# A two-layer recurrent model on one core: the gathers and joins of the second experts' rows move to later steps of the second attention

## Chip, core and metric

The kernel runs on one core of a Trainium2 chip. The metric is the device time of one execution in microseconds (us). The kernel before took 707.73 us, the median of three runs (707.6 to 710.62).

## What is computed

Two layers, one after the other, on x of shape (4, 512, 128), all in float32. Each layer normalises x, computes an attention s and a mixture of experts, turns the latter into a gate g, and adds s * g to x. The change lies in the second layer, where the experts' gate is brought together while the attention runs:

```
xn = layernorm(x)
s = L1_attn(xn, ...)            # 16 heads of 8, 16 channels of softmax attention, keys 512
g = silu(L1_ffn(xn, ...))       # each token: the two experts of largest probability out of 8
x = x + s * g

# L1_ffn, per token n:
probs = softmax(gelu(xt @ wg1 + bg1) @ wg2)
top_vals, top_idx = top_k(probs, 2)
h = gelu(einsum('nd,edh->enh', xt, w_in));  o = einsum('enh,ehd->end', h, w_out)
y[n] = sum over the token's two experts e of gate[n, e] * o[e, n]
```

## The kernel before

The tokens are four batches (b = 0 to 3) of 512, each held as a tile of 128 partitions by four groups of 128 columns (k = 0 to 3). Batch 0 runs through all eight experts densely. For batches 1 to 3 the kernel sorts tokens into rooms, one per expert, computes only the chosen experts, and writes the results as rows to a scratch table in DRAM (`rows[b]`). What comes back to each token are two rows: that of its first expert and that of its second.

`fetch(b, at)` (L1114 to L1127) brings them back. For each b there are eight gathers, at = 0 to 7, each an indirect DMA issued by GpSimd (POOL) of 128 rows of 512 bytes, one row per partition. The first four fill `g` (the first expert's rows), the last four a second tile (`first` for batch 1, `xnT` for batches 2 and 3). `joined(b, part)` (L1129 to L1135) combines them on VectorE (DVE): part 0 multiplies the first tile by its gates, part 1 the second tile by its gates, part 2 adds the two. The sum is what `gate1` (L1164) later turns into silu, and that is multiplied onto the attention's output of the same batch in `output1` (for batch 3 in `end1`).

The second attention, `attn1` (L1962), is a loop of 64 steps, i = 16 * b + t. Step i does the matmuls over one block of 128 keys of one group of four heads (`over_keys`, tile acc), evaluates the exponential and its square for step i + 1 on ScalarE (ACT) with some squares moved to DVE, and issues the scores of step i + 2 (tile s). Into the gaps it places the preparation of the following batches (projections, tiles pl, pf, feat, lin) and the mixing of finished groups (`bank1`, `sums1`, `quotients1`, `output1`, tiles b, den, mix, po). In this loop nearly everything is put on its engine in the order in which the program calls it: `mm1`, `act1`, `vec1`, `pool1` and `dma1` all pin the instruction. So an instruction that waits holds up all behind it on the same engine.

The steps that matter here:

- Whatever is in the dictionary `rest` for step i is called first in step i. It holds nothing but `fetch` and `joined`.
- What a chunk has left for DVE after its matmuls (its "rest") is called one step after the chunk's matmuls were issued. `quotients1(b - 1, 1, 0)` has its matmuls in step t = 5 and its two DVE products (L1722, tile pr) in step t = 6; `quotients1(b - 1, 1, 1)` has them in t = 6 and t = 7. Both pairs of matmuls write the tile mix, of which there are two buffers, so the second pair waits until the first pair's products have been read out by DVE.
- In step t = 4 of batch 2 (i = 36) the third part of `prepare1(3)`'s cubes and its forms (tile pl) are issued; the cubes' six DVE instructions (L1496 to L1508, tile feat) run in step 37.
- In step t = 3 the query projection of the next batch is split into three bf16 parts on POOL (L1463, L1465, tiles partq and leftq).

Before the change, batch 2's gathers stand in steps 20 to 27 and its join in steps 33 to 35; batch 3's gathers stand in steps 28 to 35 and its join in steps 50 to 52. Batch 1's are issued and joined before the loop.

Of the kernel before, what the change touches and what calls it, by code (L numbers as in the profile page):

```python
# [108 lines left out]
class Kernel:  # L109
# [2271 lines left out]
    def run(self):  # L2381
# [96 lines left out]
                self.ffn1(first, between, True)  # L2478
                third.close()
        rest = {}  # L2480
        for b, at, then in ((2, 20, 33), (3, 28, 50)):
            for k in range(8):
                rest.setdefault(at + k, []).append((first.fetch, b, k))
            for k in range(3):
                rest.setdefault(then + k, []).append((first.joined, b, k))
# [67 lines left out]
```

## Time and profile before

The profiled execution took 707.65 us, of which 705.7 us lie between its first and last instruction. The TensorE clock granted was 0.991 on the mean, and 1.00 in every stretch of ten microseconds from 420 to 700 us.

| Engine | busy, us | share of span | instructions |
|---|---|---|---|
| PE (matmul) | 662.5 | 94% | 10120 |
| DVE | 498.5 | 71% | 1072 |
| ACT | 488.9 | 69% | 809 |
| POOL | 344.7 | 49% | 383 |

| Stretch of the second attention, us | PE | DVE | ACT | POOL | DMA share |
|---|---|---|---|---|---|
| 510 to 520 | 9.98 | 8.90 | 10.00 | 8.87 | 0.49 |
| 520 to 530 | 9.48 | 9.86 | 7.85 | 8.81 | 0.47 |
| 560 to 570 | 10.00 | 10.00 | 9.03 | 6.80 | 0.72 |
| 580 to 590 | 9.60 | 9.34 | 10.00 | 7.57 | 0.68 |
| 620 to 630 | 9.90 | 7.99 | 9.03 | 3.51 | 0.27 |
| 640 to 650 | 9.07 | 8.66 | 8.90 | 1.60 | 0.87 |

How to read it: PE is a record of matmul instructions whose ends are modelled, DVE, ACT and POOL are busy times of those engines, each in us out of ten. "DMA share" is the mean busy share of the core's 16 DMA engines. An "issue" in the lists below is time in which an engine waited for nothing that the profile shows. POOL's issues of the gathers appear as DMA_INDIRECT of line L1124: their duration is the time POOL spends on the issue, not the time until the rows have arrived.

The loop's first step begins near 424 us and the last ends near 690 us, so a step takes some 4.2 us.

### The profile page before, as it was taken

Reading aid. Unit: us, or ns where it says so; the run is one execution under the profiler, and the core shown is the slowest. Engines: PE = TensorE matmul, PEld = TensorE weight load, DVE = VectorE, ACT = ScalarE, POOL = GpSimd, SP = SyncE. Lnnn points to the kernel's source line nnn. Section 1 sums busy time; section 2 is a strip of 40 time slices with the busy share of each in tenths; the row PEclk is TensorE's granted clock in tenths of the full one; section 3 lists DMA queues with packets and bytes.
Section 4 is the critical chain, followed back from the end, with each engine's and each line's share of the span. In section 5 each row is a group of like instructions: output and inputs, shape, how many; then the busy total and the mean of one; then the engine's idle time right before and its main releaser. Section 6 shows DMA issues by size and latency. Waiting matters only on the chain.

```text
span 705.7 us, 23780 instructions
## 1 busy us (share of the span) xinstructions
PE 662.5 (94%) x10120; PEld 412.4 (58%) x10123; DVE 498.5 (71%) x1072; ACT 488.9 (69%) x809; POOL 344.7 (49%) x383
## 2 busy tenths in 40 slices
PE   7999899999999799789999999999999999999995
PEld 3666667977977768767787783332335243422324
DVE  6866375676677567874459223989897999678884
ACT  4533477786876877742553468989997899899850
POOL 7670046667677384783753333411383835230170
PEclk9999999999999998999999999999999999999999
DMA  7740252232232222100034249967949494947300
GB/s 166 161 136 0 69 144 86 55 108 78 63 95 75 63 61 64 33 3 1 1 109 147 75 150 218 260 167 171 242 153 210 115 249 143 217 136 179 76 17 20
DMA packets 85489, 79.72 MB, mean 113 GB/s; under 512 B 42640, under 2 KB 74160, under 8 KB 82304
## 3 DMA queue, kind: packets, MB, share of 16 engines
q1 hardware_dynamic: 82544, 75.39, 40.4%
q0 software_dynamic: 2256, 2.47, 1.8%
q8 instruction: 82, 1.34, 0.8%
q10 hardware_dynamic: 576, 0.26, 0.1%
q14 instruction: 31, 0.25, 0.1%
HBM read 51.62 MB, written 26.21 MB: 110 GB/s over the span
## 4 chain that ended last, share of the span: by engine, by line
PE 65%; ACT 14%; DVE 12%; DMA 3%; issue 2%; SPq 1%; POOL 0%; DVEq 0%; ACTq 0%; POOLq 0%
PE acc L336 10%; ACT e L339 8%; PE eo L336 7%; PE pp L336 7%; PE po L336 5%; PE ph L336 4%; PE b L336 3%; PE s L336 3%; PE pl L336 3%; DMA vd<-vt 2%; PE pg L336 2%; PE pu L336 2%; PE den L336 2%; PE sc L336 1%; DVE elu L689 1%
## 5 line engine op out<-in xcount | busy, mean ns | idle before, releaser
L339 ACT ACTIVATE e<-s 128x1024 f32<-128x1024 f32 x124 | 121.9, 1055 | 14.0 <-PE s L336 12.9
L336 PE MATMUL acc<-e,strip 128*32 128x512 f32 x1000 | 124.5, 598 | 0.9 <-DVE e L1946 0.9
L339 ACT ACTIVATE e<-e 128x1024 f32<-128x1024 f32 x104 | 107.3, 1094 | 0.0
L743 POOL TENSOR_TENSOR t<-t,gate 128x512 f32<-128x512 f32 x32 | 50.2, 1567 | 54.9 <-DVE t L724 54.9
L336 PEld LDWEIGHTS acc<-e,strip 128*32 128x32 f32 x1000 | 28.4, 109 | 70.0 <-issue 58.3
L781 POOL TENSOR_TENSOR t<-t,gate 128x512 f32<-128x512 f32 x32 | 49.6, 1551 | 34.2 <-DVE sums L780 27.7
L689 DVE SCALAR_TENSOR_TENSOR elu<-elu,up 128x512 f32<-128x512 f32 x60 | 46.3, 771 | 11.6 <-ACT up L339 11.4
L339 ACT ACTIVATE pj<-pp 128x512 f32<-128x512 f32 x64 | 38.0, 608 | 15.4 <-PE pp L336 14.1
L339 ACT ACTIVATE h<-ph 128x1024 f32<-128x1024 f32 x20 | 20.5, 1024 | 39.0 <-PE ph L336 32.3
L336 PE MATMUL s<-q,k 64*128 64x512 bf16 x256 | 40.9, 382 | 3.6 <-ACT e L339 3.3
L782 POOL TENSOR_TENSOR t<-t,t 128x512 f32<-128x512 f32 x32 | 42.7, 1333 | 2.5
L336 PEld LDWEIGHTS <-k 64*128 64x128 bf16 x256 | 8.7, 94 | 59.7 <-issue 58.6
L666 DVE TENSOR_TENSOR E<-sc,cap 128x512 f32<-128x512 f32 x32 | 22.0, 688 | 29.5 <-PE sc L336 29.5
L336 PE MATMUL eo<-w_out,h 128*128 128x128 f32 x320 | 39.7, 278 | 0.0
L336 PEld LDWEIGHTS eo<-w_out,h 128*128 128x128 f32 x320 | 37.6, 192 | 3.4 <-issue 2.2
L339 ACT ACTIVATE elu<-pj 128x512 f32<-128x512 f32 x60 | 38.6, 643 | 0.1
L339 ACT ACTIVATE up<-pj 128x512 f32<-128x512 f32 x60 | 38.4, 640 | 0.0
L1727 POOL TENSOR_TENSOR pr<-pr,pr 128x512 f32<-128x512 f32 x14 | 22.6, 1633 | 29.7 <-DVE pr L1722 29.6
L336 PE MATMUL pp<-xnT,l0Wk 128*64 128x128 f32 x512 | 33.4, 289 | 2.4 <-ACT sk L339 1.6
L339 ACT ACTIVATE attT<-tn 128x128 f32<-128x128 f32 x100 | 19.5, 282 | 21.4 <-PE tn L702 20.5
L1634 DVE TENSOR_TENSOR second<-second,first 128x1024 f32<-128x1024 f32 x16 | 27.0, 1693 | 8.7 <-DMA second<-qf 7.3
L336 PEld LDWEIGHTS pp<-xnT,l0Wk 128*64 128x64 f32 x512 | 30.5, 146 | 4.2 <-ACT sk L339 2.6
(346 smaller groups left out, 1590.3 us busy)
## 6 DMA issues: line engine op xcount, KB each, us to landing
vd<-vt SPq DMA_DIRECT2D x32, 256.0 KB
vone<-vd SPq DMA_DIRECT2D x64, 128.0 KB
first<-qe SPq DMA_DIRECT2D x8, 1024.0 KB
second<-qf SPq DMA_DIRECT2D x16, 512.0 KB
third<-qf SPq DMA_DIRECT2D x32, 256.0 KB
qf<-qT SPq DMA_DIRECT2D x64, 64.0 KB
k<-kd SPq DMA_DIRECT2D x16, 256.0 KB
q<-qd SPq DMA_DIRECT2D x16, 256.0 KB
```

The source lines that it names most:

```text
L336: return self.pin(self.nc.tensor.matmul(*args, **kw))
L339: return self.pin(self.nc.scalar.activation(*args, **kw))
L666: self.vec1(nc.vector.tensor_tensor(e, ps[:, :, 0:256].rearrange("p x (hp c) -> p x hp c", hp=4), bc(bc(self.cap, 1, 4), 1, 2), ALU.min,))
L689: self.vec1(nc.vector.scalar_tensor_tensor(t, t, 1.0, up, ALU.min, ALU.add))
L743: nc.gpsimd.tensor_mul(t, t, self.gate)
L781: nc.gpsimd.tensor_mul(t, t, gate2)
L782: nc.gpsimd.tensor_add(t, t, seg[n]["t1"])
L1634: self.vec1(self.nc.vector.tensor_mul(t, t, self.first1[mm][:, two]))
L1727: self.nc.gpsimd.tensor_add(self.prod1[b, m], self.prod1[b, m], t)
```

## The change

One line of `run` changes: the tuples (batch, first step of its gathers, first step of its join).

```diff
         rest = {}
-        for b, at, then in ((2, 20, 33), (3, 28, 50)):
+        for b, at, then in ((2, 28, 37), (3, 44, 53)):
             for k in range(8):
                 rest.setdefault(at + k, []).append((first.fetch, b, k))
             for k in range(3):
                 rest.setdefault(then + k, []).append((first.joined, b, k))
```

Batch 2's gathers move from steps 20 to 27 to steps 28 to 35, its join from 33 to 35 to 37 to 39. Batch 3's gathers move from 28 to 35 to 44 to 51, its join from 50 to 52 to 53 to 55. No instruction is added or removed, and no tile changes its size.

In the built program POOL's order changes so: steps 20 to 27 hold no gather; in steps 28 to 35 batch 2's eight stand in exactly the places where batch 3's stood, the last one behind the five instructions that split batch 3's query projection (L1463, L1465); batch 3's first gather stands ahead of `gate1` of batch 2 (L1168), the next three behind `output1` of batch 1 (L1748), the last four behind the pair of sums L1727 that follows. On DVE, batch 2's part 0 stands between the product on tile third (L1645) and the six cubes instructions of step 37, part 1 between these and the first products pr (L1722) of step 38, part 2 between the next L1645 and the second products pr of step 39. Batch 3's parts 0 and 1 stand next to each other ahead of the products pr of step 54, part 2 ahead of those of step 55. PE, ACT and the order of SP's DMAs are as before.

## The prediction

> **What bounds the kernel now.** First the page's chain that ended last, by engine:
>
> ```profile
> PE 65%; ACT 14%; DVE 12%; DMA 3%; issue 2%; SPq 1%; POOL 0%; DVEq 0%; ACTq 0%; POOLq 0%
> ```
>
> POOL, which issues the gathers, is not on it. TensorE is, and DVE in places, so I ask where DVE decides, and whether the moved joins land there. The same chain in order of time for 580 to 592 us (start, us, what), and DVE's timeline there (start, us, engine, line, operation; in brackets idle time before and its releaser):
>
> ```profile
> 580.92 1.51 PE pl L336 x64
> 582.43 0.02 issue
> 582.45 2.16 DVE feat L1496
> ...
> 585.37 2.40 DVE feat L1508 x3
> 587.76 0.60 DVE pr L1722
> ...
> 588.41 1.72 PE mix L336 x4
> ```
>
> ```profile
> 580.55 1.27 DVE L1645 SCALAR_TENSOR_TENSOR third<-second,count,third 128x1024 f32<-128x1024 f32 x1
> 582.45 2.16 DVE L1496 TENSOR_TENSOR feat<-tokk,feat 128x1024 f32<-128x1024 f32 x1 [0.63 <-PE pl L336]
> ```
>
> This is steps 37 and 38. Six cubes instructions and a product pr run back to back on DVE, and PE's second mix stands behind that pr. After it PE goes without a gap to 617 us. So whatever DVE does between 582.45 and 587.76 moves the end. Exactly there the change puts batch 2's parts 0 and 1.
>
> Third, when part 1's rows arrive. Their last gather takes the place of batch 3's last one; POOL's timeline:
>
> ```profile
> 586.46 0.69 POOL L1463 CAST partq<-leftq 128x512 bf16<-128x512 f32 x1
> 587.30 0.98 POOL L1124 DMA_INDIRECT xnT<-rows,ids  x1 [0.15 <-issue]
> ```
>
> Its rows' packets show in stretches of a quarter of a microsecond (busy PE, PEld, DVE, ACT, POOL, clock, DMA share, GB/s). The clearest case is the last gather before the loop, issued at 395.88 us with little traffic around; the second pair belongs to the gather at 587.30:
>
> ```profile
> 397.25:397.50 0.25, 0.07 (x2) 0.00 (x0) 0.00 (x0) 0.25 (x2) 0.00 (x0) 1.00 0.00 0
> 397.50:397.75 0.25, 0.01 (x1) 0.00 (x0) 0.00 (x0) 0.25 (x1) 0.00 (x0) 1.00 0.81 246
> ```
> ```profile
> 588.75:589.00 0.25, 0.25 (x2) 0.00 (x0) 0.25 (x2) 0.25 (x1) 0.25 (x1) 1.00 0.32 74
> 589.00:589.25 0.25, 0.25 (x3) 0.24 (x2) 0.25 (x1) 0.25 (x1) 0.25 (x1) 1.00 1.97 184
> ```
>
> 246 GB/s for 0.25 us is 61 KB, the 64 KB of one gather: packets run 1.62 to 1.9 us after the issue starts, near 589.25 for the other. DVE reaches the spot at 587.76. **The rows come too late for it.**
>
> **The change, part by part.**
>
> *Part 1 of batch 2 waits (step 38).* The packets' end is not yet the semaphore. At the kernel's start two loads of 64 KB end near 2.9 us, and the first DVE instruction that waits for one starts at 3.34, so I add 0.5 (between 0.4 and 0.8): a gather can be used 1.95 + 0.5 = 2.45 us after its issue starts. The Trainium skill, "DMA: Bandwidth & Descriptors", section on the anatomy of a SWDGE DMA, gives 2.0 us fixed plus bytes over 436 GB/s, which for 64 KB would be an estimated 2.15 us; by it the wait is 0.3 shorter. I take the row.
>
> *Part 0 (step 37).* Each join is one product of 0.68 us (rows L1131: 0.68, 0.68, 0.69 when undisturbed). It stands behind the L1645 that ends at 581.82, in the 0.63 us for which DVE waits for pl: by that, 0.05 lost. But POOL splits the query then, and "SBUF — State Buffer", section "Who interferes with whom", says that a DVE instruction with two SBUF inputs and a POOL instruction reading SBUF exclude each other. The trace has it: L1131 took 1.64 us at 570.31 beside POOL's leftk, and L1496 2.16 at 582.45 against 1.21 at 566.04. If part 0 is served between the first cast and the first subtraction, both queues behind it shift by about 0.65. I take 0.65, with 0 and 1.0 as ends.
>
> *Sum at step 38.* Gather issue 587.30 + 0.65 = 587.95; usable at 587.95 + 2.45 = 590.40; part 1 itself 0.60 from start to start, so pr starts at 591.0 in place of 587.69: **+3.3 us**. Without part 0's shift and with the skill's figure it is 587.30 + 2.15 + 0.60 - 587.69 = +2.4; with part 0 at 1.0, and the issue held up by DVE as at 530.87 us (1.97 in place of 0.98), +4.6. Had the rows been there, part 1 would cost 0.6 alone. Behind the waiting instruction stand both pr pairs, sizes and all of DVE; PE's mix waits for the first pr, and acc, the scores and ACT's next exponentials wait behind mix. ACT can run on for some 4 us (it holds one step of scores) and then waits too. PE and then ACT (617 to 623) are the chain behind it, so nothing absorbs the loss.
>
> *Part 2 (step 39)* adds 0.6 between L1645 (589.72) and pr (590.91). The pr behind it frees mix for pf, 4.8 us after the first pr; with 0.6 more it is done after some 4.5. Cost 0, but only 0.3 us of cover.
>
> *What leaves steps 33 to 35.* Three joins (564.84, 570.31, 574.62), while PE runs without a gap and is the chain: 0.
>
> *What leaves steps 50 to 52.* Here DVE is the chain:
>
> ```profile
> 638.97 1.13 DVE first L1643
> 640.10 0.60 DVE xnT L1131
> 640.70 1.67 DVE inv L1695
> ...
> 642.45 1.15 DVE e L1946
> 643.59 0.04 issue
> 643.64 1.05 PE acc L336 x4
> ```
>
> Batch 3's part 1 leaves it: -0.6. Part 0 (633.74) stood before 1.71 us of waiting for den: 0. Part 2 (643.49) stood where ACT takes over: 0. ACT's gap there is 1.10 us, so the gain ends at 1.1; beyond it ACT is late next. **-0.6.**
>
> *What enters steps 53 to 55.* Parts 0 and 1 follow the L1645 that ends at 647.40; DVE then waits 1.34 us for mix (to 648.73). 2 x 0.68 = 1.36 fits: 0. Part 2 stands before the pr of 653.08; ACT is the chain from 645.97 to 657.25 and DVE waits 0.35 at 657.23 and 1.55 at 660.00: 0, or 0.3 at most. Its rows, last issued by about 634 us, have 13 us.
>
> *POOL and DMA.* Eight gathers leave 515 to 530 us, eight enter between 610 and 634. Alone one takes 0.95, with 0.30 between (386.90 to 396.8): 8 x 1.25 = 10 us. The SBUF page of the skill, section "SBUF: two separate sides", speaks against them: the descriptors of such a DMA can't be written while DVE holds the shared port, and this stretch of DVE is 80% busy; the worst here is 1.97, so 18 us. POOL was idle 16.57, 2.61, 5.65 and 13.92 us before its instructions from 610.76 to 642.59; th and L1764 have that cover, so 0 by either. If a gather did delay th, y would follow, but its output is only stored. The half megabyte goes where the DMA share was 0.27 (620 to 630 us); the tables loaded from 629.5 on are first used at 646.12 (third). SP's order is unchanged. In steps 28 to 35 one batch replaces the other, gather for gather.
>
> **Sum:** 3.3 - 0.6 = +2.7, on 707.65 us (the execution profiled, 0.08 under the median of 707.73): 710.35. I forecast **710.3**, own range 709.3 to 712.0.
>
> **Rivals.**
>
> *Not slower: the gathers slowed PE.* PE loses 0.52 us at 521.92, then 1.66 in b and 0.55 in acc (527.79 to 532.9): 2.7 us that no releaser explains.
>
> ```profile
> 527.79 2.72 PE L336 MATMUL b<-third,lin 64*32 64x512 f32 x16
> 530.45 2.47 PE L336 MATMUL acc<-e,strip 128*32 128x512 f32 x16
> ```
>
> Elsewhere these take 1.06 and 1.92. Nine gathers are issued from 515.27 to 532.84, and PE's gaps at 397.31 and 397.96 follow the last of batch 1's. Against it: the gathers from 552.96 to 564.6 have no such mark, and a gap of 0.67 at 85.97 has no gather near. If the gathers are the cause, 2.7 comes back: 707.65 + 2.7 - 2.7 = 707.7. It decides as soon as it returns more than 2.7; with the rows early as well (cost 0.6 + 0.05, not 3.3) 705.0. Chance 0.19.
>
> *Clearly slower: the gather meets a full DMA.* kd's parts, issued until 572.91, let POOL go on only at 581.32, under a DMA share of 1.0: 8.4 us instead of 2.45, so +6 more, 716. The share at 588 to 590 is 0.72, and 0.26 afterwards, which speaks against it. It decides from 1 us of extra landing time (711.3). Chance 0.25, mostly for 1 to 3 us.
>
> *The wait is hidden:* DVE reaches part 1 later or the rows come sooner; then only 0.65 + 0.6 - 0.6 remain: 708.3. Chance 0.11.
>
> The forecast keeps 0.45. What a measurement here can tell from no change is about 0.5%, or 3.5 us: 704.2 to 711.3. Forecast, hidden wait and most of PE's recovery fall within it; slower are the full-DMA case and the forecast's upper end (0.03). Faster is PE's recovery with early rows (0.05), so same is 0.67, slower 0.28. The range for 8 in 10: 707.0 to 713.5.
>
> **What will show it.** Right: DVE idle about 2 us before xnT L1131 near 588.4, released by a DMA; PE's mix about 3.3 later than 588.41, everything to 636 shifted equally, 0.6 won back at acc near 643.64. Wrong: xnT L1131 without idle time before it, or PE's b near 527 at 1.06 per tile.

## The result, and the profile after

The changed kernel took 711.52 us in the median of 19 runs (709.86 to 714.23); the kernel before, measured beside it, took 707.56 us (19 runs, 704.96 to 710.62). The ratio is 1.0062, with a 95% interval from 1.005 to 1.0074: about 4 us slower. The profiled execution of the changed kernel took 711.52 us, 709.5 of them span, against 707.65 and 705.7 before.

The page's chain that ended last, by engine, after the change. DMA stood at 3% before:

```profile
PE 61%; ACT 15%; DVE 13%; DMA 5%; issue 3%; POOL 1%; SPq 1%; DVEq 0%; ACTq 0%; POOLq 0%
```

Where the new share lies is seen in the same chain in order of time, of the changed kernel (start, us, what), up to the matmuls of step 38:

```profile
568.51 11.37 DMA kd<-partk
...
584.35 0.69 POOL partq L1463
585.04 0.15 issue
585.20 3.51 DMA xnT<-rows,ids
...
588.82 0.69 DVE xnT L1131
589.52 0.61 DVE pr L1722
...
590.17 2.67 PE mix L336 x4
592.84 3.15 PE acc L336 x16
```

Before, this stretch was DVE work without a gap. Now it runs through a transfer that POOL's split of the query waits for (kd, 11.37 us, the larger part of the new DMA share), the split, the last gather (3.51 us) and part 1 of the join. DVE's timeline of the changed kernel shows the wait itself (in brackets the idle time before and who ended it):

```profile
579.31 1.10 DVE L1131 TENSOR_TENSOR g<-g,gates 128x512 f32<-128x512 f32 x1
580.67 1.84 DVE L1496 TENSOR_TENSOR feat<-tokk,feat 128x1024 f32<-128x1024 f32 x1 [0.27 <-PE pl L336]
...
583.19 2.47 DVE L1508 TENSOR_TENSOR feat<-tokk,feat 128x256 f32<-128x256 f32 x3
588.82 0.69 DVE L1131 TENSOR_TENSOR xnT<-xnT,gates 128x512 f32<-128x512 f32 x1 [3.17 <-DMA xnT<-rows,ids]
589.43 1.28 DVE L1722 TENSOR_TENSOR pr<-bank,mix 128x512 f32<-128x512 f32 x2
```

Two rows of PE's timeline hold what nothing in the prediction answers to. First the two rows before the change, then those of the changed kernel:

```profile
588.41 1.72 PE L336 MATMUL mix<-inv,to_mix 64*128 64x512 f32 x4 [0.40 <-DVE pr L1722]
590.06 1.92 PE L336 MATMUL acc<-e,strip 128*32 128x512 f32 x16
```
```profile
590.17 2.67 PE L336 MATMUL mix<-inv,to_mix 64*128 64x512 f32 x4 [3.93 <-DVE pr L1722]
592.77 3.22 PE L336 MATMUL acc<-e,strip 128*32 128x512 f32 x16
```

PE waited 3.93 us and then ran slower: mix took 2.67 us in place of 1.72, acc 3.22 in place of 1.92. The stretches of that window show why (busy PE, PEld, DVE, ACT, POOL, then the granted clock, DMA share, GB/s):

```profile
588.00:588.50 0.50, 0.00 (x0) 0.00 (x0) 0.00 (x0) 0.50 (x2) 0.00 (x0) 1.00 0.30 111
588.50:589.00 0.50, 0.00 (x0) 0.00 (x0) 0.18 (x1) 0.50 (x2) 0.00 (x0) 0.62 0.28 107
589.00:595.00 6.00, 4.83 (x16) 1.59 (x20) 5.96 (x10) 2.41 (x3) 0.97 (x1) 0.50 0.26 96
595.00:595.50 0.50, 0.50 (x8) 0.00 (x0) 0.47 (x3) 0.00 (x0) 0.50 (x2) 0.55 0.26 102
```

While PE stood idle its clock fell to 0.50, and it stayed there for 6.8 us (0.38 of the second row, 6.00, and 0.45 of the last, if the clock is either 1.00 or 0.50), most of them after PE had gone on.

Starts of the same PE blocks in the two profiles give the account. The third column is another execution of the changed kernel (last experiment below), on another chip:

| PE block (start before, us) | changed kernel, shift | second profile of it, shift |
|---|---|---|
| mix at 513.09 | +0.25 | +0.41 |
| pl at 533.39 | -1.79 | -1.64 |
| mix at 584.48 (step 37) | -1.78 | -1.63 |
| mix at 588.41 (step 38) | +1.76 | +2.55 |
| pf at 592.46 (step 39) | +4.00 | +5.51 |
| b at 597.26 (step 40) | +4.55 | +5.51 |
| den at 634.15 | +4.55 | +5.52 |
| mix at 647.67 (step 53) | +3.74 | +4.71 |
| mix at 676.27 | +3.96 | +4.94 |

So the changed kernel loses 3.5 us to the wait, 2.2 to the halved clock and 0.55 in pl and acc behind it. It gains 2.0 between 513 and 533, where PE's slow stretch is gone, and 0.8 at steps 50 to 52, of which 0.2 is lost again at step 54.

### The profile page after: what moved, and what is told of

The parts are those of the page before. It is cut to its first block, busy times and chain, and to the rows that moved or that the text cites. A ratio compares the mean times of both kernels' runs of the same rounds, so it can differ in the third digit from the quotient of the medians.

```text
span 709.5 us, 23785 instructions
## 1 busy us (share of the span) xinstructions
PE 661.3 (93%) x10120; PEld 410.7 (58%) x10123; DVE 498.6 (70%) x1072; ACT 489.5 (69%) x809; POOL 346.0 (49%) x383
## 3 DMA queue, kind: packets, MB, share of 16 engines
q0 software_dynamic: 2256, 2.47, 1.8%
## 4 chain that ended last, share of the span: by engine, by line
PE 61%; ACT 15%; DVE 13%; DMA 5%; issue 3%; POOL 1%; SPq 1%; DVEq 0%; ACTq 0%; POOLq 0%
PE acc L336 8%; ACT e L339 8%; PE eo L336 7%; PE pp L336 7%; PE po L336 5%; PE ph L336 4%; PE b L336 3%; PE s L336 3%; PE pl L336 2%; DMA vd<-vt 2%; PE pu L336 2%; PE pg L336 2%; DMA kd<-partk 2%; PE sc L336 1%; DVE elu L689 1%
## 5 line engine op out<-in xcount | busy, mean ns | idle before, releaser
L1727 POOL TENSOR_TENSOR pr<-pr,pr 128x512 f32<-128x512 f32 x14 | 22.5, 1630 | 35.4 <-DVE pr L1722 35.3
L336 PE MATMUL pp<-xnT,l0Wk 128*64 128x128 f32 x512 | 31.2, 275 | 3.3 <-ACT sk L339 2.0
L336 PE MATMUL pp<-xnT,l0Wq 128*64 128x128 f32 x512 | 31.8, 284 | 2.4 <-ACT sk L339 2.1
```

What stands on the lines that cost most here:

```text
L336: return self.pin(self.nc.tensor.matmul(*args, **kw))
L1727: self.nc.gpsimd.tensor_add(self.prod1[b, m], self.prod1[b, m], t)
```

## The experiments

The runs came in four groups. Each group ran on one chip, with runs of the kernel before between them, and the chips differ: the kernel before took 707.59 us in the first group, 706.92 in the second, 702.99 in the third and 709.14 in the fourth. So times are compared within a group, or as ratios to the kernel before of the same group. In the diffs below the minus line is that of the changed kernel.

My theory was that the rows of batch 2's last gather come too late for the join. Its rival was that the join's place on DVE costs the time by itself.

### First group: late rows, or the join's place?

**Gathers early, join where the change put it.**

```diff
-        for b, at, then in ((2, 28, 37), (3, 44, 53)):
+        for b, at, then in ((2, 20, 37), (3, 44, 53)):
```

> Batch 2's gathers go back to steps 20 to 27, its join stays in steps 37 to 39, batch 3 stays as changed. Theory of the late rows: the rows have landed long before step 38, so DVE doesn't wait, the clock stays at full, and only part 0 (0 to 0.65 us) and part 1 (0.6 us) remain, less the 0.6 won in batch 3: some 0.7 us over before, near 708.2. Rival, the join's place itself (three more DVE instructions ahead of the products that PE's mix waits for) costs the time: as slow as the changed kernel, near 711.5.

Measured: 708.14 us, ratio 1.0012 [0.9999, 1.0025]. DVE doesn't wait before part 1, PE's second mix waits 1.50 us in place of 3.93, and the clock stays at 1.00. That mix still comes 1.13 us later than before: part 1 of the join stands ahead of it, and so does a slower L1508 (3.31 us in place of 2.48; the run with the last gather alone says more on that). The times of the two kernels differ by 3.4 us, and that difference goes with the place of the gathers.

**Join late, gathers where the change put them.**

```diff
-        for b, at, then in ((2, 28, 37), (3, 44, 53)):
+        for b, at, then in ((2, 28, 39), (3, 44, 53)):
```

> Gathers as in the changed kernel, batch 2's join two steps later, in steps 39 to 41. Theory of the late rows: no wait on the rows, PE's gap before the second mix is back to some 0.4 us, the 0.6 of batch 3 is kept: 706.5 to 708, at or under the kernel before. If the gathers in steps 20 to 27 also slow PE (they are gone here too), 2 us less again, near 705. Rival, the join anywhere behind step 37 is on the path: over 709.

Measured: 705.58 us, ratio 0.9966 [0.9952, 0.998]: faster than both kernels. DVE's timeline of this kernel shows step 37 and 38 as they were before, with part 0 of the join only in step 39:

```profile
585.72 2.46 DVE L1508 TENSOR_TENSOR feat<-tokk,feat 128x256 f32<-128x256 f32 x3
588.11 1.27 DVE L1722 TENSOR_TENSOR pr<-bank,mix 128x512 f32<-128x512 f32 x2
...
591.34 0.68 DVE L1131 TENSOR_TENSOR g<-g,gates 128x512 f32<-128x512 f32 x1
```

Both edits remove the wait, one from each side, and with either the loss is gone or nearly so.

**Batch 3's part alone.**

```diff
-        for b, at, then in ((2, 28, 37), (3, 44, 53)):
+        for b, at, then in ((2, 20, 33), (3, 44, 53)):
```

> Only batch 3's part of the change: batch 2 as before (20, 33), batch 3 at 44 and 53. Expected: DVE's chain in steps 50 to 52 is shorter by one product, 0.6 us: 707.0. If batch 3's gathers in steps 44 to 51 cost anything, or its join in steps 53 to 55, it is at or over 707.6.

Measured: 707.52 us, ratio 0.9997 [0.9978, 1.0015]. The times can't resolve 0.6 us. The trace shows it: PE's blocks stand 0.8 us earlier after steps 50 to 52 than ahead of them, and 0.2 of this is lost again at step 54 (b starts 10.11 us after the first mix there, 9.90 before). The trace also shows a price: step 35 holds no gather in this kernel, L1508 takes 3.3 us in place of 2.48, and PE's mix of step 38 comes 0.5 us later.

**PE kept busy through the wait.** The scores of step 40, which PE issues ahead of the awaited mix, are written twelve times over in two of their four parts:

```diff
-        for r in range(4):
+        for r in list(range(4)) + [2, 3] * (12 if i == 40 else 0):
```

> The changed kernel, with the last two of the four score matmuls of step 40 repeated twelve times (24 matmuls that write the same values again, some 2.6 to 3.2 us), so that PE works during most of its wait in step 38. Theory of the clock: the granted clock doesn't fall to 0.5, and the second mix and the sums behind it take 1.72 and 1.85 us again in place of 2.67 and 3.15: 2 us under the changed kernel, near 709.3, though there is more work. Rival, the clock's fall costs nothing or has another cause: 711.5 or above.

Measured: 709.89 us, ratio 1.004 [1.0024, 1.0057]. The time came near what was expected, but not by the mechanism expected: PE still waited 1.88 us behind the repeats, and the clock fell all the same, for 3.4 us in place of 6.8, and only at 590.78 us, when PE had been working again for 1.3 us. PE's timeline of this kernel, and its stretches of one microsecond:

```profile
584.29 3.33 PE L336 MATMUL s<-q,k 64*128 64x512 bf16 x28
589.50 2.02 PE L336 MATMUL mix<-inv,to_mix 64*128 64x512 f32 x4 [1.88 <-DVE pr L1722]
591.45 3.26 PE L336 MATMUL acc<-e,strip 128*32 128x512 f32 x16
```
```profile
590.00:591.00 1.00, 1.00 (x4) 0.29 (x2) 0.96 (x4) 0.57 (x1) 0.00 (x0) 0.89 0.25 98
591.00:592.00 1.00, 1.00 (x5) 0.20 (x8) 1.00 (x2) 0.00 (x0) 0.00 (x0) 0.50 0.26 100
```

So this run didn't settle the clock's part, and a second dose was needed.

### Second group: one gather, and a PE that never idles

**The kernel before, profiled again.**

> The kernel before, unchanged, for a second profile. Open is whether the slow stretch of PE between 522 and 533 us (b 2.72 in place of 1.06, acc 2.47 in place of 1.92, some 2 us in all) belongs to the gathers in steps 20 to 27. If it does, it is there again, b third above 1.6 us. If it is a chance event of one execution, the stretch is at 1.06 and 1.92 and the span about 2 us shorter.

One execution, 706.0 us. The slow stretch came back smaller. PE's timeline of this second execution of the kernel before:

```profile
527.06 1.13 PE L336 MATMUL b<-third,lin 64*32 64x512 f32 x16
528.12 2.56 PE L336 MATMUL acc<-e,strip 128*32 128x512 f32 x16
```

The tile b takes 1.13 us here (2.72 in the first profile), but acc takes 2.56 where 1.92 is usual, and 0.2 are lost behind it. From the mix at 513 to the den at 538 this execution wins 1.54 us on the first. So the size of that stretch is different in each execution, and neither expectation fits.

**Only the last gather one step earlier.**

```diff
-                rest.setdefault(at + k, []).append((first.fetch, b, k))
+                rest.setdefault(at + k - (b == 2 and k == 7), []).append((first.fetch, b, k))
```

> The changed kernel with one instruction moved: the last of batch 2's eight gathers is issued in step 34 in place of step 35, so ahead of the split of the query projection on POOL; join unchanged in steps 37 to 39. If the late rows of this one gather are the whole loss: no wait on a DMA before part 1, first pr about 0.6 to 1.2 us later than in the kernel before, TensorE's clock stays at 1.00, and the time is about 706.5, between the kernel with the join at 39 (705.6) and that with the early gathers (708.1). If the place of the join on DVE costs it: 710 or more.

Measured: 707.49 us, ratio 1.0007 [0.9998, 1.0017], 1 us above what was expected. One gather of eight, moved ahead of POOL's split, brings the kernel back to the time before. DVE's timeline of this kernel has no wait left before part 1:

```profile
583.87 3.31 DVE L1508 TENSOR_TENSOR feat<-tokk,feat 128x256 f32<-128x256 f32 x3
587.11 0.68 DVE L1131 TENSOR_TENSOR xnT<-xnT,gates 128x512 f32<-128x512 f32 x1
```

What it keeps of the loss shows here too. L1508 takes 3.31 us in place of 2.47, with POOL's product tokq (L1396) now beside it and no gather issued between the split and tokq. All fourteen profiles agree on that, here and near 513 us: without a gather in between some 3.3 us, with one 2.46 to 2.48. PE waited 1.64 us for mix, and behind that gap the clock fell for 3.4 us: PE's blocks shift by 1.65 us more from mix to pf. The fall came at 590.07 us, 1.6 us after PE had gone on. In the kernel with early gathers a gap of 1.50 us had no such effect.

**Batch 2's part alone.**

```diff
-        for b, at, then in ((2, 28, 37), (3, 44, 53)):
+        for b, at, then in ((2, 28, 37), (3, 36, 50)):
```

> Batch 2's part of the change alone: gathers in 28 to 35, join in 37 to 39; batch 3's gathers in 36 to 43, its join in 50 to 52 as before. If the loss is batch 2's alone and batch 3's part wins 0.6 at steps 50 to 52: 711.5 + 0.6 = 712.1, with the wait before part 1 and the clock at 0.50 again. If batch 3's late gathers or late join cost something: below 711.0.

Measured: 716.86 us (6 runs), ratio 1.0124 [1.0092, 1.0156]: the wait is there (3.52 us on DVE), the clock falls for 6.8 us, and some 5 us come on top that I hadn't expected. They are not there each time: two of the six runs took 711.84 and 712.43, as expected, the other four 716.5 to 718.4, and the profile is one of these four. The chain of this kernel in order of time shows where:

```profile
598.34 1.24 PE pl L336 x52
599.58 0.22 issue
599.80 0.44 PE pl L336 x4
600.24 0.41 issue
600.66 0.42 PE pl L336 x4
601.08 0.29 issue
601.37 0.29 PE pl L336
```

PE stalls again and again in its short matmuls of pl, for nothing that a releaser explains, while POOL issues four gathers from 597.01 to 602.57; between pf and b 3.9 us are lost. That is the picture of the slow stretch before, and a first hint that gathers issued beside such short matmuls can hold PE up.

**PE filled to the end of the wait:** the same edit with 20 in place of 12.

> The changed kernel with the same two score matmuls of step 40 repeated 20 times (40 matmuls of 0.115 us, 4.6 us) in place of 12, so that PE is busy until the awaited product pr comes at about 589.5 us; the repeats write the same values again. If the clock's fall costs the 2.2 us and needs an idle PE: clock 1.00 throughout 584 to 600 us, PE's gap before mix below 0.5 us, time 709.3 or less. If such half-array matmuls don't count as activity for the clock: it falls again, and the time is 710 or more. If the clock has nothing to do with it: 711.5.

Measured: 709.67 us, ratio 1.0041 [1.0027, 1.0056]. PE's timeline of this kernel:

```profile
585.91 5.06 PE L336 MATMUL s<-q,k 64*128 64x512 bf16 x44
590.85 1.72 PE L336 MATMUL mix<-inv,to_mix 64*128 64x512 f32 x4
592.50 1.93 PE L336 MATMUL acc<-e,strip 128*32 128x512 f32 x16
```

The wait on DVE is as long as ever (3.44 us), but PE has no gap, the clock stays at 1.00, and mix and acc are back at 1.72 and 1.93. From mix to b nothing more is lost, where the changed kernel lost 2.8. So here the halved clock came from the idle PE: with work in its place, and the wait unchanged, the clock stayed up. The expected time was put on a base of 707.6 us; on this group's 706.92 it would be 708.6, and 709.67 is 1 us above it, though below the 710 of the other theory. The loss of 2.75 us is close to what the trace has for the wait alone, 3.8, less 0.6 at steps 50 to 54 and the 0.5 that the slow stretch still cost in this chip's profile of the kernel before.

### Third group: do gathers hold PE up?

**The faster version once more,** the one with the join at step 39.

> The kernel with gathers in 28 to 35 and 44 to 51 and joins at 39 to 41 and 53 to 55 once more, as the base of the next two. Expected as measured before: 705.6, 0.3% under the kernel before; no PE gap before the second mix of step 38, clock 1.00 there.

Measured: 702.23 us, ratio 0.9989 [0.998, 0.9998]. It is ahead of the kernel before on this chip as well, but by 0.8 us, not by 2.0.

**Batch 2's gathers in both places.**

```diff
-        for b, at, then in ((2, 28, 37), (3, 44, 53)):
+        for b, at, then in ((2, 28, 39), (3, 44, 53)):
             for k in range(8):
                 rest.setdefault(at + k, []).append((first.fetch, b, k))
+                if b == 2:
+                    rest.setdefault(20 + k, []).append((first.fetch, b, k))
```

> That kernel with eight gathers more: batch 2's rows are also fetched in steps 20 to 27, where the kernel before fetches them, and then again in 28 to 35, so the first eight are surplus. If gathers in 20 to 27 hold up PE: its tiles pl, b and acc between 516 and 534 us lose 1.0 to 2.9 us as in four profiles with gathers there, 0.85 of that comes back since POOL's tokq no longer stands beside DVE's L1508, and the time is 705.8 to 707.6, 706.6 as the middle. If the gathers there are harmless and the slow stretch is an accident: 705.6 or 0.8 less.

Measured: 702.36 us, 0.13 above its base; ratio 0.9995 [0.9984, 1.0006]. Eight gathers more in steps 20 to 27 cost nothing that can be measured here, as the second expectation had it. In the trace b takes 1.23 us three times where its base has 1.09, 1.06 and 1.06, which makes 0.35 up to pl; against that, L1508 near 511 us takes 2.46 in place of 3.31 and mix starts 0.7 to 0.8 sooner.

**Batch 2's part alone, without the wait.**

```diff
-        for b, at, then in ((2, 28, 37), (3, 44, 53)):
+        for b, at, then in ((2, 28, 39), (3, 36, 50)):
```

> That kernel with batch 3's gathers in steps 36 to 43 in place of 44 to 51 and its join at 50 to 52 as before, so batch 2's part of the change alone, with the join that doesn't wait. It tells what made the kernel with batch 2's part alone so slow (716.9, where 712.1 was expected). If gathers in 36 to 43 hold up PE in its dense tiles pl and acc near 600 us by themselves (3.9 us there): 705.6 + 0.6 + 3.9 = 710.1. If that loss comes only behind the late rows and the halved clock: 706.2.

Measured: 704.08 us, 1.85 above its base. In the trace 0.86 us are lost from mix to b of steps 38 to 40 (0.37 of them in pl and acc) and 0.6 at steps 50 to 54, where batch 3's part 1 is back on DVE's chain. So the 3.9 us of the earlier run are not the fixed price of these gathers; neither expectation fits.

### Fourth group: the changed kernel again

> The changed kernel once more, for a second profile and a second comparison. If the late rows and the halved clock are its fixed price: a wait on a DMA of about 3.2 us before part 1, the clock at 0.50 for six to seven us from about 2.5 us after PE goes idle, and a ratio to the kernel before of 1.005 to 1.008. If the clock's fall was an accident of the one profiled execution: clock 1.00 and a ratio near 1.003.

Measured: 711.84 us against 709.14, ratio 1.0044 [1.0028, 1.006], just under the lower end of what was expected; the profiled execution took 712.55. The wait and the clock's fall are there again, but the fall came 4.5 us after PE went idle, just as PE took up work, and not 2.5. DVE's and PE's timelines of this execution:

```profile
579.46 0.69 DVE L1131 TENSOR_TENSOR g<-g,gates 128x512 f32<-128x512 f32 x1
580.83 2.12 DVE L1496 TENSOR_TENSOR feat<-tokk,feat 128x1024 f32<-128x1024 f32 x1 [0.68 <-PE pl L336]
...
589.62 0.69 DVE L1131 TENSOR_TENSOR xnT<-xnT,gates 128x512 f32<-128x512 f32 x1 [3.53 <-DMA xnT<-rows,ids]
```
```profile
590.96 2.67 PE L336 MATMUL mix<-inv,to_mix 64*128 64x512 f32 x4 [4.54 <-DVE pr L1722]
593.56 3.64 PE L336 MATMUL acc<-e,strip 128*32 128x512 f32 x16
```

## Why the prediction was right, and where it was not

The predicted time was 710.3 us, on a base of 707.65; measured were 711.52, within the forecast's own range of 709.3 to 712.0. The change itself was forecast at +2.65 us and measured at +3.96. Direction and main mechanism hold, but the nearness of the sum is partly luck: terms that were missing have both signs.

| Term | predicted, us | profile after | second profile |
|---|---|---|---|
| gather issue later in its step (part 0) | +0.65 | -0.3 | 0.0 |
| gather issue until its rows can be used | 2.45 | 3.62 | 3.99 |
| first pr of step 38 later | +3.3 | +3.5 | +4.2 |
| clock behind the idle PE | not named | +2.2 | +3.0 |
| pl and acc near 599 us | not named | +0.55 | 0 |
| steps 50 to 52 | -0.6 | -0.8 | -0.8 |
| steps 53 to 55 | 0, 0.3 at most | +0.2 | +0.2 |
| PE between 513 and 533 us | 0 in the sum | -2.0 | -2.0 |

*Part 1 waits.* Shown. DVE stood idle for 3.17 us before xnT L1131, released by the DMA, and PE's mix came 3.5 us later. Where the rows no longer came after the join's place, the loss went or nearly went: with early gathers, with a late join, and with the last gather alone moved.

*How long a gather takes.* This term was mis-sized. I took 2.45 us: packets over after 1.95, and 0.5 from the last packet to the waiting engine. From issue to use it was 3.62, 3.89, 3.91, 3.98 and 3.99 us in the five profiles with the wait. The error lies in how the stretches were read. Those of the changed kernel, the gather being issued at 585.20, look as predicted:

```profile
587.00:587.25 0.25, 0.00 (x0) 0.00 (x0) 0.00 (x0) 0.25 (x1) 0.25 (x1) 1.00 2.05 172
587.25:587.50 0.25, 0.00 (x0) 0.00 (x0) 0.00 (x0) 0.25 (x2) 0.00 (x1) 1.00 0.21 41
```

But a DMA share of 2.05 is more than all 16 engines: this view counts a packet whole in the stretch in which it starts. The view of the DMA queues, asked for 587.5 to 588.3 us, still has 21 packets of the gathers' own queue that start there (packets, MB, share of 16 engines):

```profile
q0 software_dynamic: 21, 0.02, 10.0%
```

The trace's packet records of that queue have the ends as well. The 32 packets of this gather start from 587.05 on, and the last ends at 588.25, 3.05 us after the issue; DVE starts 0.57 us behind it. In the three profiles e4, e8 and e12 the packets end 3.2 us after the issue and DVE starts 0.7 to 0.8 later. So the 0.5 was nearly right, and the 1.95 was not. It was wrong already for the rows that the prediction reads: the packets of the gather issued at 587.30 before the change run from 589.13 to 590.55, those of the undisturbed one issued at 395.88 from 397.53 to 398.06, so they end 3.25 and 2.18 us after their issue. The estimate of 2.15 us, worked out from the Trainium skill, "DMA: Bandwidth & Descriptors", section on the anatomy of a SWDGE DMA, was further off.

*Part 0.* The 0.65 that I added for it was wrong as well: it took 1.10 us in the one profile and 0.69 in the other, L1496 behind it took 1.84 and 2.12, and POOL's gather was issued no later in its step than before. This error and the one before it cancel in part.

*The clock.* This is the step that failed: a term left at nothing. "PE and then ACT (617 to 623) are the chain behind it, so nothing absorbs the loss" counts PE's wait once, as if PE went on afterwards as before. It didn't. The prediction's own numbers made PE idle for 3.7 us (0.4 + 3.3), and the Trainium skill, "TensorE: Matmul & The Clock Gate", section "Part 1: The HAM clock gate", says that about 3.4 us of an idle window bring the clock down to half, and about 3.4 us of work bring it back. By this rule some 3.4 us at half clock, a loss of about 1.7, an estimate from that page, belonged in the sum, which would then have been 712. The traces agree on the length: half clock lasted 6.8 us, two such windows, in the three profiles with a gap of 3.9 to 4.5 us, and 3.4 us, one window, in two with gaps of 1.6 and 1.9. They don't agree on the condition: those two gaps are shorter than the rule asks for, and in the profile after the clock fell when PE had been idle for 2.38 us. The loss is 2.2 us in that profile and 3.0 in the second, since 1.55 us of half clock fell into the wait in the one and none in the other. With PE filled the clock didn't fall. That the fall costs the 2 to 3 us that PE's rows show is read from those rows. The times don't separate it: the ratios of the filled kernels (1.004 and 1.0041) lie below the first one of the changed kernel (1.0062) and beside its second (1.0044).

*Steps 50 to 52 and 53 to 55.* The net of -0.6 came as worked out, from two terms that were each 0.2 off: 0.8 is won at steps 50 to 52, and 0.2 is lost at step 54 in each of the profiles with joins at 53 to 55 (10.1 us from the first mix there to b, 9.9 with the joins at 50 to 52). *Part 2 at step 39* cost nothing, as worked out: from mix to pf it is 4.04 us with early gathers and with PE filled, 4.05 before. *POOL:* batch 3's moved gathers took 0.95 to 1.97 us each to issue, and POOL was still idle for 16.84 us before th, so they held up nothing that PE waits for. The section "SBUF: two separate sides" that the prediction names there states the lock for DVE operations in a two-port mode; which of DVE's instructions made some issues longer, no run tests.

*PE's slow stretch* was the rival "not slower", at 2.7 us. In the nine profiles without gathers in steps 20 to 27 it was absent, b at 1.06 among them, which the prediction had named as a sign against itself; in the five with gathers it had any size from some 0.35 (third group) to 2.9 us. So gathers beside PE's short matmuls take part in it, but with them gone only a part comes back: another part is lost on L1508 (3.31 in place of 2.46). In the times it was worth at most 1.9 us on one chip (join late against batch 3 alone, which differ by the 0.5 us at step 38 too) and 0.1 on another. Why it varies so, and why batch 2's part alone lost 3.9 us in such a place, stays open.

*The full DMA* didn't come with its 6 us, but in a milder form it did. The prediction gave this case 0.25, mostly for 1 to 3 us more, and 711.3 for 1 us; the rows came 1.2 to 1.5 us later than the 2.45. Part of that lies in the packets: they took 1.2 us from the first start to the last end in the profile after, single ones up to 1.12, where those of the undisturbed gather took 0.53 and single ones up to 0.29. That the other transfers of that moment stretched them is likely, since the DMA share just ahead was 0.9 to 1.0, but no run tests it.

The sum of the second profile (+4.9 on the first profile of the kernel before) is larger than that group's difference of medians, 2.7. The two profiles come from different chips, on which the kernel before took 707.56 and 709.14, and this execution lay 0.7 above its own median; the rest is not accounted for.

## What to carry to other kernels

Before moving the join of a gather, count from the gather's issue to the instruction that uses it with a latency measured on a gather that somebody waits for, or at least from the ends of its packets and not from the stretch in which they start. Here it was 3.6 to 4.0 us, and moving one gather by a step, or the join by two, removed the loss or nearly all of it. A wait that reaches PE is to be priced twice: the wait, and the clock behind it. And where the wait can be passed by placing the join later, the same move of the gathers becomes a small gain: with the join at step 39 the kernel was faster than both, at ratios of 0.9966 and 0.9989.

## What the runs showed of the hardware

- A gap of 1.6 or 1.9 us was enough for the clock to fall in two profiles, though 1.50 us was not in a third. Nor is a gap always needed: the kernel before has a fall at 266.41 us although PE's record is full from 255 us on. Among its matmuls in the last 3 us ahead of that fall are 16 of only 8 columns (lp, 1.95 us by the record), so a PE that is busy by the record may not count as one; no run tests this.
- Within one profile the granted clock changes only at times that lie whole multiples of 3.413 us apart: after the change at 243.88, 247.29, 588.62 and 595.45 us, which are 1, 100 and 2 such steps. Where this grid lies differs from execution to execution. PE's matmuls pp behind a gap of 2.06 us near 242 us took 4.51 us, mostly at a clock of 0.50, in the profile after, where the gap lies whole in one step of the grid, and 2.84 in the profile before, where a step's end at 242.52 cuts it into 0.63 and 1.43. This may be why the same code loses the clock in one execution and not in another, but it is not the whole rule: in the run with gathers in both places 2.00 us of that gap lie in one step, and the clock stayed up.
- Between the end of a gather's last packet and the start of the instruction that waited for it lay 0.57 to 0.78 us in four profiles, against 0.4 read for plain loads at the kernel's start. The packets themselves ended 3.05 to 3.2 us after the issue.
- The chips differ by up to 6 us in the same kernel (702.99 to 709.14), and in how much PE loses beside gathers.
